# The per-column maximum of a softmax, taken in 32 by 32 blocks on VectorE instead of by five transposes on TensorE

## The chip, the cores and the metric

The kernel runs on one core of one Trainium2 chip. The metric is device time in microseconds of one launch, taken as the median of several runs. One execution was recorded by the hardware profiler, and every duration below comes from that execution.

## The reference, cut to what matters

The whole is one decoder-like layer of three parts (cross-attention with fp8-rounded projections, a small ternary attention with its feed-forward part, a gated feed-forward part). What the change touches is the cross-attention over a long context:

```python
x        : (16, 64, 256)      # 16 batches of 64 queries
ctx_2048 : (16, 1601, 256)    # 16 batches of 1601 context rows
kvx = einsum('bsi,oi->bso', cond, w_kv_x)            # keys and values of the context
kx, vx = split(kvx, 2, axis=-1); kx = _ln(kx ...)    # layer norm over each key head (8 heads of 128)
qx = _ln(_fp8_linear_pertensor(ln_out, wqx, ...))    # 16 query heads, two to a key head
xout = _gqa(qx, kx, vx)                              # softmax(q k / sqrt(128)) v over the 1601 rows
```

The softmax subtracts a maximum, and that maximum is what is computed in another way.

## The kernel before, in words

**Tiles.** The 1024 rows of x are 8 tiles of 128 rows (two batches each). The long attention of a tile is cut into four units: two halves of the heads (hh) times two batches (bb). So there are 32 units, and each walks over 13 chunks of the context (12 of 128 rows and a tail of 65). A unit covers 8 query heads of 64 queries, which makes 512 columns, in four groups g of 128 columns.

**A chunk's way.** `project` (L620) multiplies the context by the key weights on TensorE. ScalarE squares (L555) and splits the keys for a transposing DMA (L647, L651, L661). VectorE sums the squares (`roots`, L560), GpSimd takes the inverse root (L563, L564). `score` (L692, TensorE) makes the scores with context rows on the partitions and the 512 columns along the free axis; ScalarE copies them to a tile P with the inverse root as scale (L702). `running` (L711, VectorE) keeps the running maximum M, a 128 by 512 tile, over the chunks. After the tail chunk `biased_maximum` (L723) adds a bias row to M.

**From M to one maximum for each column.** M still holds 128 partial maxima for each column, one on each partition. `maximum` calls `turned` (L713 to L720): four transposes on TensorE (L717) turn M's four 128 by 128 groups into one PSUM tile tr_m, and VectorE reduces it to 128 by 4, `red` (L719). `out_rows` (L431 to L437) then turns `red` with a fifth transpose (tr_r, L434), ScalarE copies the 4 by 128 result to SBUF (rT, L436), and SyncE's queue writes it to DRAM (rowd, L437). `maximum_in` (L740) reads it back, broadcast to all 128 partitions, as mx. Only the last of the 32 units goes another way: it transposes `red` four more times with broadcast (L734) and uses no DRAM.

**What uses the maximum.** `shifted` (L746, L750, VectorE) adds the negated maximum to each of the 13 stored P tiles, `exponent` (L754, ScalarE) takes the exponential, `accumulate` (L769, TensorE) multiplies by the context. That begins one step after `maximum_in` is issued.

**What sets the order.** A heap of generators with step and rank (`at`, `spawn`, `run`) writes the program in an order laid out by hand; a unit takes 13 steps. The tile framework then places each engine's instructions in a queue of its own, where they run in order, and lets an instruction be moved a little among its neighbours. `ordered("dve", ...)` forbids such a move on VectorE among L560, L711, L723 and L750. `maximum` stands at step 16 of its unit, rank 4.0, after the `project` of that step (rank 2.5) and before its `accumulate` (rank 4.5).

**Buffers.** The score tiles, tr_m, tr_r and most other small PSUM tiles share one tag of three buffers (`tr_tile`, `s_tile`). M has one buffer. `quant_tile()` gives a 128 by 512 scratch tile of two buffers (q_y), used so far by the fp8 rounding, the layer norm of a tile and the query bias on GpSimd (L413).

Of the kernel before, what the change touches and what calls it, by code (L numbers as in the profile page):

```python
# [14 lines left out]
F32 = mybir.dt.float32  # L15
# [5 lines left out]
AX = mybir.AxisListType  # L21
PSUM = bass.MemoryType.PSUM

P = 128
# [49 lines left out]
def body(tc, ctx, a):  # L74
    nc = tc.nc
    V, A, PE, GP = nc.vector, nc.scalar, nc.tensor, nc.gpsimd

    const = ctx.enter_context(tc.tile_pool(name="const", bufs=1))
    small = ctx.enter_context(tc.tile_pool(name="small", bufs=8))
# [6 lines left out]
    dram = ctx.enter_context(tc.tile_pool(name="dram", bufs=2, space=bass.MemoryType.DRAM))  # L86
# [4 lines left out]
    def tr_tile(name, dt=F32):  # L91
        return ps_s.tile([P, 512], dt, tag="s", name=name)
# [7 lines left out]
    def spawn(step, rank, gen):  # L100
        heapq.heappush(heap, (step, rank, next(count), gen))
# [14 lines left out]
    def at(step, rank, fn):  # L116
        def once():
            fn()
            yield 1

        spawn(step, rank, once())
# [22 lines left out]
    ident = const.tile([P, P], F32, tag="ident", name="ident")  # L144
# [85 lines left out]
    def quant_tile():  # L230
        return qp.tile([P, 512], F32, tag="q_y", name="q_y")
# [199 lines left out]
    def out_rows(r, d):  # L431

        tr = tr_tile("tr_r")
        PE.transpose(tr[0:4, 0:P], r, ident)  # L434
        rT = small.tile([4, P], F32, tag="rT", name="rT", bufs=2)
        A.copy(rT, tr[0:4, 0:P])  # L436
        nc.sync.dma_start(out=d, in_=rT)  # L437
# [102 lines left out]
    def behind(ins, other):  # L540

        tc.add_manual_dep(
            ins.ins, other.ins.name,
            mybir.DependencyInfo(mybir.DependencyClass.NoSync, mybir.DependencyReason.DATA), reason="order",
        )

    def ordered(chain, ins):

        if chain in mark:
            behind(ins, mark[chain])  # L550
        mark[chain] = ins
# [41 lines left out]
    def unit(i, hh, bb, base):  # L593
        b = 2 * i + bb
        last, u = b == B - 1 and hh == 1, 4 * i + 2 * hh + bb
        st = {"kh": {}, "kd": {}, "kt": {}, "cxT": {}, "cxN": {}, "ps": {}, "ss": {}, "rs": {}, "kn": {}, "kT": {}, "P": {}, "pT": {}}
# [116 lines left out]
        def turned(what, op):  # L713

            tr = tr_tile("tr_m")
            for g in range(4):
                PE.transpose(tr[:, g * P : (g + 1) * P], st[what][:, g * P : (g + 1) * P], ident)  # L717
            r = small.tile([P, 4], F32, tag="red", name="red")
            V.tensor_reduce(r, tr.rearrange("p (g t) -> p g t", g=4), AX.X, op)  # L719
            return r  # L720

        def biased_maximum():
            ordered("dve", V.tensor_tensor(st["M"], st["M"], st["qb"].rearrange("p h s -> p (h s)"), ALU.add))  # L723

        def maximum():
            r = turned("M", ALU.max)
            if not last:
                st["mxd"] = dram.tile([4, P], F32, tag="rowd", name="rowd", bufs=4)
                out_rows(r, st["mxd"])
                return  # L730

            tr = tr_tile("tr_mb")
            for g in range(4):
                PE.transpose(tr[:, g * P : (g + 1) * P], r[:, g : g + 1].to_broadcast([P, P]), ident)  # L734
            st["mx"] = one.tile([P, 4, P], F32, tag="mx", name="mx", bufs=2)
            A.copy(st["mx"], tr.rearrange("p (g q) -> p g q", g=4))

        def maximum_in():
            st["mx"] = one.tile([P, 4, P], F32, tag="mx", name="mx", bufs=2)
            nc.sync.dma_start(out=st["mx"], in_=st["mxd"].partition_broadcast(P))  # L740

        def shifted(c):
            n, pc = rows_of(c), st["P"][c]
# [12 lines left out]
        def accumulate(c):  # L756


            n = rows_of(c)
            if c == 0:  # L760
                st["acc"] = [ps_acc.tile([P, 512], F32, tag=f"acc{k}", name=f"acc{k}") for k in range(3)]
            pc, cx, acc = st["P"].pop(c), st["cxN"].pop(c), st["acc"]

            for t in acc[:2] if c == 0 else []:
                PE.matmul(t[:, 0:386], lhsT=zeros[:, 0:P], rhs=zeros, start=True, stop=False)
            for g, o, ps in [(0, 0, acc[0][:, 0:257]), (1, 0, acc[1][:, 0:257]), (2, 0, acc[2][:, 0:257]),
                             (3, 0, acc[0][:, 257:385]), (3, P, acc[1][:, 257:386])]:
                w = ps.shape[1]
                PE.matmul(  # L769
                    ps, lhsT=pc[:n, g * P : (g + 1) * P], rhs=cx[:n, o : o + w], start=g == 2 and c == 0,  # L770
                    stop=c == NC - 1 and (g, o) in ((2, 0), (3, 0), (3, P)),
                )
            if c == NC - 1:
                acc = st.pop("acc")
                rv = small.tile([P, 4], F32, tag="rvx", name="rvx", bufs=2)
                pq = one.tile([P, 4, H], F32, tag="pq", name="pq")
                for g, s in enumerate([acc[0][:, 256:257], acc[1][:, 256:257], acc[2][:, 256:257], acc[1][:, 385:386]]):
                    V.reciprocal(rv[:, g : g + 1], s)
                A.activation(pq[:, 0, :], acc[0][:, 0:256], AF.Copy, scale=rv[:, 0:1])
                V.tensor_scalar(pq[:, 1, :], acc[1][:, 0:256], rv[:, 1:2], None, ALU.mult)  # L780
                A.activation(pq[:, 2, :], acc[2][:, 0:256], AF.Copy, scale=rv[:, 2:3])
                V.tensor_scalar(pq[:, 3, P:H], acc[1][:, 257:385], rv[:, 3:4], None, ALU.mult)
                V.tensor_scalar(pq[:, 3, 0:P], acc[0][:, 257:385], rv[:, 3:4], None, ALU.mult)
                st["pq"] = pq
# [15 lines left out]
        for c in range(NC):  # L800
# [20 lines left out]
            at(base + c + 19, 3.7, lambda c=c: exponent(c))  # L821
            at(base + c + 20, 4.5, lambda c=c: accumulate(c))
        at(base + 15, 5.2 + 0.01, biased_maximum)
        at(base + 16 if not last else base + 15, 4.0, maximum)
        if not last:
            at(base + 17, 5.4, maximum_in)
# [429 lines left out]
    for i in range(NT):  # L1256
        base = 52 * i
        for hh in range(2):
            for bb in range(2):
                unit(i, hh, bb, base + 26 * hh + 13 * bb)  # L1260
            spawn(base + 26 * hh + 13 + 34 - 2 + (2, 1)[hh], 6.5, paced("pair", pair_out(i, hh, 4 if i < NT - 1 or hh == 0 else None)))
        ln0, sa0, qx0 = SCHEDULE[i] if i in SCHEDULE else (
            base - 22, [base + o for o in (-15, 0, 8, 21)], [base + o for o in (-16, -7, 15, 18)]
        )
        spawn(ln0, 1.0, paced("ln" if i else "ln_first", ln_tile(i)))
        for p in range(4):
            spawn(sa0[p] - 2, 5.0, paced("sa", self_attention(i, p)))
            spawn(qx0[p] - 2, 3.0, paced("qx", queries(i, p)))
        l0 = base + {NT - 3: 95, NT - 2: 88, NT - 1: 82}.get(i, 90)
        spawn(l0, 4.5, paced("last" if i < NT - 1 else "last_tile", last_parts(i, l0)))  # L1270
# [79 lines left out]
```

## Time and profile before

| | |
|---|---|
| median of 3 runs | 2410.33 us (2405.0 to 2416.17) |
| the profiled execution, its own time | 2408.62 us |
| its span, first to last instruction | 2406.8 us |
| mean granted TensorE clock | 0.991 |
| TensorE matmul, busy | 2333.5 us (97%) |
| TensorE weight load, busy | 1764.1 us (73%) |
| VectorE, busy | 1842.2 us (77%) |
| ScalarE, busy | 1730.2 us (72%) |
| GpSimd, busy | 825.1 us (34%) |

Abbreviations of the profile: PE is TensorE's matmul side, PEld its weight loads, DVE is VectorE, ACT ScalarE, POOL GpSimd, SP SyncE, and SPq SyncE's DMA queue. L717 is line 717 of the kernel before. The matmuls of fp32 operands show as two records each (two passes), the fp32 transposes as one. A matmul's record contains its way through the array, so the records of neighbouring matmuls overlap; how fast TensorE goes is read from start to start, not from durations. "Idle before" is the time in which the group's engine had nothing to do just ahead of it, with the releaser that ended it.

### The profile page before, as it was taken

To read this page: it belongs to the slowest core of one execution; us is meant where nothing else is said; L and a number is where in the kernel's file an instruction comes from. 1 tells how busy PE (TensorE), PEld (TensorE's weight loads), DVE (VectorE), ACT (ScalarE), POOL (GpSimd) and SP (SyncE) were. 2 spreads that over 40 slices of the span, in tenths; PEclk is the share of its full clock that TensorE was granted. 3 is DMA by queue.
4 is the path that set the end of the run, shared out by engine and by line. 5 is a ranking of instruction groups with operands and counts; after the bars stand their busy time and mean duration, and the time that the engine had idled before them with its cause. 6 is when DMAs were issued, how large, how long until landed. Compare 5 with 4: busy or idle time off the path is not lost.

```text
span 2406.8 us, 40362 instructions
## 1 busy us (share of the span) xinstructions
PE 2333.5 (97%) x12541; PEld 1764.1 (73%) x12541; DVE 1842.2 (77%) x4515; ACT 1730.2 (72%) x3789; POOL 825.1 (34%) x1017
## 2 busy tenths in 40 slices
PE   7999999999999999999999999999999999999995
PEld 4577777777777777777777777777777777677774
DVE  7677768878777887687877778777887777876765
ACT  4677777777887777977788777777687777767631
POOL 3333233333343433343433433324434343332200
PEclk9999999999999999999999999999999999999997
DMA  8989868777977689686987769877797767965323
GB/s 262 260 242 254 231 173 242 203 185 188 267 201 199 167 237 232 184 214 181 233 220 193 200 174 256 207 191 189 183 263 199 201 169 190 261 160 140 116 85 110
DMA packets 683661, 485.17 MB, mean 202 GB/s; under 512 B 464476, under 2 KB 592952, under 8 KB 683448
## 3 DMA queue, kind: packets, MB, share of 16 engines
q1 hardware_dynamic: 682904, 481.91, 74.2%
q8 instruction: 100, 1.64, 0.3%
q14 instruction: 113, 0.93, 0.1%
q10 hardware_dynamic: 544, 0.69, 0.1%
HBM read 271.03 MB, written 113.11 MB: 160 GB/s over the span
## 4 chain that ended last, share of the span: by engine, by line
PE 69%; DVE 11%; issue 6%; DMA 5%; POOL 4%; ACT 4%; SPq 1%; ACTq 0%; DVEq 0%; POOLq 0%
PE acc L769 21%; PE ps_k L620 21%; PE s L692 12%; PE po_x L856 2%; PE po_p L325 2%; POOL rsx L564 2%; POOL rs L219 2%; PE ps_q L374 1%; ACT P L702 1%; DMA kd<-kh 1%; DMA wqx<-wqx 1%; DMA kT<-kd 1%; DVE P L750 1%; DVE M L711 1%; PE tr_pc L792 1%
## 5 line engine op out<-in xcount | busy, mean ns | idle before, releaser
L769 PEld LDWEIGHTS acc<-ctxN,P 128*128 128x128 f32 (+1 forms) x4160 | 712.3, 190 | 221.7 <-issue 143.0
L769 PE MATMUL acc<-ctxN,P 128*128 128x257 f32 (+5 forms) x4160 | 803.0, 339 | 4.7 <-DMA ctxN<-in_ctx_n 2.2
L620 PE MATMUL ps_k<-wkx,ctxT 128*128 128x512 f32 x1600 | 759.7, 596 | 8.1 <-DVE wkx L1243 6.4
L702 ACT ACTIVATE P<-s,rsx 128x128 f32<-128x128 f32 x1536 | 441.1, 373 | 159.5 <-PE s L692 144.1
L563 POOL TENSOR_SCALAR vx<-ss 128x4 f32<-128x4 f32 x402 | 145.6, 362 | 1112.5 <-DVE ss L560 785.4
L564 POOL TENSOR_TENSOR rsx<-vx,nhalf 128x4 f32<-128x4 f32 x402 | 471.2, 1172 | 32.8 <-POOL vx L563 0.2
L620 PEld LDWEIGHTS ps_k<-wkx,ctxT 128*128 128x128 f32 x1600 | 276.8, 191 | 201.9 <-issue 185.6
L692 PE MATMUL s<-qx,kT 128*128 128x128 f32 x3072 | 411.7, 277 | 6.3 <-DMA kT<-kd 2.7
L692 PEld LDWEIGHTS s<-qx,kT 128*128 128x128 f32 x3072 | 377.5, 192 | 24.5 <-issue 6.6
L711 DVE TENSOR_TENSOR M<-P,M 128x512 f32<-128x512 f32 (+1 forms) x384 | 264.2, 688 | 156.5 <-ACT P L702 143.6
L647 ACT COPY kh<-ps_k 128x1024 uint16<-128x1024 uint16 x360 | 366.8, 1019 | 3.3 <-DMA kd<-kh 3.1
L754 ACT ACTIVATE P<-P 128x512 f32<-128x512 f32 (+1 forms) x416 | 266.3, 640 | 123.6 <-DVE P L750 121.2
L555 ACT ACTIVATE sq<-ps_k 128x512 f32<-128x512 f32 x402 | 242.8, 604 | 151.3 <-PE ps_k L620 124.6
L560 DVE TENSOR_REDUCE ss<-sq 128x4 f32<-128x512 f32 x402 | 272.3, 677 | 34.1 <-ACT sq L555 32.7
L750 DVE TENSOR_TENSOR P<-P,mx 128x512 f32<-128x512 f32 (+1 forms) x416 | 283.4, 682 | 0.0
L219 POOL TENSOR_TENSOR rs<-ve,nhalf 128x4 f32<-128x4 f32 (+2 forms) x128 | 128.7, 1007 | 278.1 <-DVE ve L218 263.1
L225 DVE TENSOR_SCALAR qn<-qn,mv,rs 128x128 f32<-128x128 f32 x256 | 77.4, 344 | 49.9 <-POOL rs L219 49.0
L303 DVE TENSOR_TENSOR wproj<-wproj,w_hi 128x1024 fp32r<-128x1024 f32 x60 | 72.8, 1216 | 9.0 <-ACT w_hi L302 9.0
L215 DVE BATCH_NORM_STATS2 st<-qn 128x6 f32<-128x128 f32 x256 | 64.5, 271 | 17.8 <-ACT qn L384 17.8
L413 POOL TENSOR_TENSOR q_y<-qn,brow 128x512 f32<-128x512 f32 x32 | 58.5, 1827 | 49.8 <-DVE qn L225 35.2
L302 ACT CAST w_hi<-wproj 128x1024 fp32r<-128x1024 f32 x60 | 63.3, 1056 | 8.5 <-DMA wproj<-wproj 5.4
L325 PE MATMUL po_p<-wproj,cat 128*128 128x256 f32 x272 | 67.0, 293 | 0.0
(234 smaller groups left out, 2871.4 us busy)
## 6 DMA issues: line engine op xcount, KB each, us to landing
kd<-kh SPq DMA_DIRECT2D x375, 256.0 KB
ctxT<-in_ctx SPq DMA_DIRECT2D x192, 256.0 KB
ctxN<-in_ctx_n SPq DMA_DIRECT2D x384, 128.0 KB
wproj<-wproj SPq DMA_DIRECT2D x68, 512.0 KB
wq<-wq SPq DMA_DIRECT2D x32, 512.0 KB
wkv<-wkv SPq DMA_DIRECT2D x32, 512.0 KB
wqx<-wqx SPq DMA_DIRECT2D x32, 512.0 KB
near<-kv SPq DMA_DIRECT2D x248, 64.0 KB
```

Of the source, the lines that this page charges most:

```text
L219: GP.tensor_tensor(rs[:, :g], ve[:, :g], nhalf[:, :g], ALU.pow)
L555: A.activation(sq[:n], ps[:n], AF.Square)
L560: ordered("dve", V.reduce_sum(ss[:n], sq[:n].rearrange("p (g d) -> p g d", g=4), axis=AX.X))
L564: ordered("pool", GP.tensor_tensor(rs[:n], ve[:n], nhalf[:n, 0:4], ALU.pow))
L620: PE.matmul(ps[:n, :], lhsT=st["cxT"][c // 2][:, k, o : o + n], rhs=wkx[:, k, 512 * hh : 512 * (hh + 1)], start=k == 0, stop=k == 1,)
L647: A.copy(t, src.bitcast(U16).rearrange("p (c e) -> p e c", e=2))
L692: PE.matmul(ps[:n, g * P : (g + 1) * P], lhsT=kT[:, g, 0:n], rhs=qxs[i, hh][:, bb, 2 * g : 2 * g + 2, :].rearrange("p h s -> p (h s)"), st ...
L702: A.activation(pc[:, g * P : (g + 1) * P], ps[:, g * P : (g + 1) * P], AF.Copy, scale=rs[:, g : g + 1])
L711: ordered("dve", V.tensor_tensor(st["M"][:n], pc[:n], st["M"][:n], ALU.max))
L750: ordered("dve", V.tensor_tensor(pc[:n], pc[:n], st["mx"][:n].rearrange("p g q -> p (g q)"), ALU.add))
L754: A.activation(pc[:n], pc[:n], AF.Exp)
L769: PE.matmul(ps, lhsT=pc[:n, g * P : (g + 1) * P], rhs=cx[:n, o : o + w], start=g == 2 and c == 0, stop=c == NC - 1 and (g, o) in ((2, 0), ...
```

## The change

VectorE's transpose turns each 32 by 32 block of M in place in the grid, so that the 32 partitions of a block become its 32 free columns. One reduce over the inner 32 then gives r16: for each of four bands of partitions and each of 16 blocks, the maximum of the band, with the 32 columns of the block on the partitions. One transpose on TensorE (r16, 128 by 16) puts the 16 blocks on partitions and the four bands side by side. A last small reduce takes the maximum over the four bands, straight from PSUM into the 16 by 32 tile that the DMA writes to DRAM. The broadcast read back is the same 2 KB for each partition. The last unit is left as it was.

For each of 31 units, four 128 by 128 transposes on TensorE, the 128 by 512 reduce L719 and ScalarE's copy rT go; VectorE gets the transpose and the reduce in `blocks`, directly behind L723 in its ordered chain, and the reduce rmx in `maximum`; the fifth transpose stays, with r16 in place of `red`.

```diff
         def biased_maximum():
             ordered("dve", V.tensor_tensor(st["M"], st["M"], st["qb"].rearrange("p h s -> p (h s)"), ALU.add))
 
+        def blocks():
+            if last:
+                return
+            t = quant_tile()
+            ordered("dve", V.transpose(t, st["M"]))
+            st["r16"] = small.tile([P, 16], F32, tag="r16", name="r16", bufs=2)
+            ordered("dve", V.reduce_max(st["r16"], t.rearrange("p (f t) -> p f t", f=16), axis=AX.X))
+
         def maximum():
+            if not last:
+                tr = tr_tile("tr_m")
+                PE.transpose(tr[0:16, 0:P], st["r16"], ident)
+                r = small.tile([16, 32], F32, tag="rmx", name="rmx", bufs=2)
+                V.reduce_max(r, tr[0:16, 0:P].rearrange("p (b q) -> p q b", b=4), axis=AX.X)
+                st["mxd"] = dram.tile([16, 32], F32, tag="rowd", name="rowd", bufs=4)
+                nc.sync.dma_start(out=st["mxd"], in_=r)
+                return
+
             r = turned("M", ALU.max)
-            if not last:
-                st["mxd"] = dram.tile([4, P], F32, tag="rowd", name="rowd", bufs=4)
-                out_rows(r, st["mxd"])
-                return
...
         def maximum_in():
             st["mx"] = one.tile([P, 4, P], F32, tag="mx", name="mx", bufs=2)
-            nc.sync.dma_start(out=st["mx"], in_=st["mxd"].partition_broadcast(P))
+            nc.sync.dma_start(
+                out=st["mx"].rearrange("p g (f q) -> p (g f) q", f=4), in_=st["mxd"].partition_broadcast(P)
+            )
...
         at(base + 15, 5.2 + 0.01, biased_maximum)
+        at(base + 15, 5.2 + 0.02, blocks)
         at(base + 16 if not last else base + 15, 4.0, maximum)
```

## The prediction

> **What bounds the kernel now.** First the page: busy shares, then the slices.
>
> ```profile
> PE 2333.5 (97%) x12541; PEld 1764.1 (73%) x12541; DVE 1842.2 (77%) x4515; ACT 1730.2 (72%) x3789; POOL 825.1 (34%) x1017
> ...
> PE   7999999999999999999999999999999999999995
> ...
> DVE  7677768878777887687877778777887777876765
> ...
> PEclk9999999999999999999999999999999999999997
> ```
>
> TensorE is busy nearly without a break at an almost full clock, VectorE about three quarters. A busy TensorE may only be waiting in its own pipeline, so second, the waits of TensorE in the stretch from 120 to 2280 us, longest first (total, times, longest):
>
> ```profile
> PE ps_g L1105 <- ACT w_hi L302: 3.0, 3, 1.3
> PE s L692 <- DMA kT<-kd: 2.7, 5, 1.7
> PE acc L769 <- DMA ctxN<-in_ctx_n: 2.2, 3, 0.9
> PE s L692 <- ACT P L702: 2.1, 6, 0.5
> ```
>
> Nothing holds TensorE for more than 3 us in 2160. Third, start to start: successive passes of 128 columns begin 0.109 us apart, of 257 columns 0.216, of 512 columns 0.429. I took each start-to-start gap of the trace, less that interval: the excess is 145 us in the whole span, of which 31 us lie before 120 us and 36 after 2280. Between, it is some 2.2 us in 60, so there TensorE goes at its own pace, and what is taken off its queue is taken off the span.
>
> The Trainium skill ("Perfetto Trace Analysis", Identifying the Most-Contended Engine) warns of just this reading: matmul busy time is a poor measure, weight-load share and the other engines' occupancy a better one. By it VectorE (77%) stands above TensorE (73%), and a change that loads VectorE would lose time (rival C below gives how much). The row here that decides is start to start, and it says TensorE.
>
> Fourth, the timeline of one unit (start, duration, engine, what):
>
> ```profile
> 800.33 0.69 DVE L723 TENSOR_TENSOR M<-M,qb 128x512 f32<-128x512 f32 x1
> ...
> 800.94 0.68 DVE L750 TENSOR_TENSOR P<-P,mx 128x512 f32<-128x512 f32 x1
> ...
> 803.43 0.60 PE L717 MATMUL tr_m<-ident,M 128*128 128x128 f32 x4
> ...
> 803.87 1.03 PE L769 MATMUL acc<-ctxN,P 128*128 128x257 f32 x4
> 804.07 0.69 DVE L719 TENSOR_REDUCE red<-tr_m 128x4 f32<-128x512 f32 x1 [1.65 <-PE tr_m L717]
> ...
> 804.91 0.27 PE L434 MATMUL tr_r<-ident,red 128*4 128x128 f32 x1
> ...
> 805.02 1.04 PE L769 MATMUL acc<-ctxN,P 128*128 128x257 f32 x6
> ```
>
> M is ready at 801.02, TensorE comes to tr_m at 803.43: VectorE is 2.4 us ahead. The four transposes take 803.87 - 803.43 = 0.44 us of the queue. Four passes of acc (4 x 0.216 = 0.86) follow, so tr_r could start at 804.73; it starts at 804.91, since it waits for `red`: 0.17 us of standstill.
>
> **The change part by part.** In the built order of TensorE's queue nothing moves but these instructions (and two key matmuls by some places): one tr_m of 128 by 16 stands where the four stood, and tr_r is gone.
>
> Removed on TensorE: 31 units x 4 x 0.109 = 13.5 us. The new transpose costs what tr_r cost (next start 0.109 us later, stationary 4 columns; 16 columns I take as the same), so the fifth cancels. Also removed: the standstill before tr_r. Summed over the 31 units it is 7.2 us: 2.1 in the first unit, mostly 0.08 or 0.17 in the others. Together 20.7 us.
>
> The new wait: tr_m now needs r16, not M, and behind tr_m in TensorE's queue wait acc and all that follows. The groups that price it (busy, mean ns, idle before and its releaser):
>
> ```profile
> L560 DVE TENSOR_REDUCE ss<-sq 128x4 f32<-128x512 f32 x400 | 271.0, 677 | 33.7 <-ACT sq L555 32.4
> L750 DVE TENSOR_TENSOR P<-P,mx 128x512 f32<-128x512 f32 x384 | 261.7, 682 | 0.0
> L303 DVE TENSOR_TENSOR wproj<-wproj,w_hi 128x1024 fp32r<-128x1024 f32 x60 | 72.8, 1216 | 9.0 <-ACT w_hi L302 9.0
> L719 DVE TENSOR_REDUCE red<-tr_m 128x4 f32<-128x512 f32 x32 | 21.9, 685 | 32.8 <-PE tr_m L717 32.8
> L709 DVE COPY M<-P 128x512 f32<-128x512 f32 x32 | 13.4, 419 | 3.8 <-ACT P L702 3.8
> ```
>
> A VectorE transpose is not in this trace. From below, the fastest row of that shape is the copy L709, 0.42 us; from above, the row with twice the elements, L303, 1.22. I take 0.68 (L750, L711, L560): most rows of 512 fp32 elements have it. The reduce in `blocks` is L560's shape, 0.68. Neighbours on VectorE start 0.08 us before the last one ends (800.33 + 0.69 against 800.94), so each adds 0.60, and tr_r began 0.06 to 0.15 after `red` ended. r16 is thus usable 0.60 + 0.60 + 0.1 = 1.3 us after M.
>
> From the end of L723 to the first tr_m the trace has 0.15 us in two units, 1.53 to 1.54 in five, 1.76 in one, 2.3 or more in 23 (median 3.2). In the first of the two, a weight scaling (0.39) stands between in the built order, so tr_m waits 1.55 us; in the other 1.15. In the five, two small steps (L218, L225; 0.14 and 0.26) come between, so 1.7 is needed against 1.53: 0.2 each, 1.0 in all. The rest waits for nothing. New waits: 3.7 us. With the transpose at 1.22, eight units pay 0.54 more at most, 4.3 us; at 0.42, 1.8 us less.
>
> The Trainium skill ("VectorE: DVE Perf Modes", The three transpose paths; Rules for kernel authors) gives 311 ns for 128 by 128 bf16 on VectorE, sends 128 by 128 transposes to TensorE, and calls the reduce the slowest VectorE operation. Four times 311 ns would be 1.24 us, an estimate, and the time 2398 instead of 2394; the rows show the reduce (677 ns) no slower than the sum of two tensors (682).
>
> VectorE's load: + 0.68 (transpose) + 0.68 (r16) + 0.29 (rmx; L1060 reduces 128 elements in 0.286, L491 256 from PSUM in 0.42) - 0.69 (`red`) = 0.96 us a unit, 30 us over 31, to about 1872. I cost this at nothing. Cover one: VectorE now stands idle 32.8 us in front of `red`, waiting for tr_m; the 1.2 us put in front of that falls into the idle time in the 22 units that have it. Cover two: behind `blocks` in the queue are the shift L750, the sum of squares L560 and the copy L510. From the end of a shift, its exponential allowed for, to its acc there are 8 us in the median, 1.8 at the first percentile; from L510 to its po_s at least 1.6. Both exceed 1.2. If the cover were gone: 31 x 1.2 = 37 us. The new user of q_y has two buffers whose earlier readers are mostly on VectorE itself, ahead of it; one buffer wait on GpSimd's product (1.8 us) would be the most in a unit.
>
> ScalarE loses 31 copies of 0.25 us, 8 us; it is idle 28%, so nothing comes of it. rowd: SyncE's queue waits for rmx instead of rT, behind it stand kd, kT and ctxN. rmx can end about 0.7 us after tr_m starts, rT ended 2.04 us after it (805.47 against 803.43), so that wait gets shorter. The write has 16 rows of 128 bytes for 4 of 512; the read back is 128 by 512 in the built order as before. VectorE waited for mx 4.8 us in all, so the landing has room.
>
> Sum: - 13.5 - 7.2 + 3.7 = - 17 us. The profiled execution took 2408.6 (span 2406.8 and 1.8 around it), so 2391.6; the median lies 1.7 higher: 2410.3 - 17 = 2393.3, say 2394.
>
> **The rivals.**
>
> B, the gain half lost, 2402 us: the transpose takes 1.22 us (4.3 more), and later VectorE steps hold TensorE for another 4, for instance at the s matmuls, which already have 20 us of small waits. For it: the operation's price is unknown. Against: the slacks above. It counts as no change, since 0.5%, 12 us, is about what a measurement of this kernel can tell.
>
> C, slower, 2427 us: VectorE's queue decides after all. Its place is tr_m waiting for r16 and, behind it, everything VectorE hands on late; if the 1.2 us passes whole to TensorE in each unit, it is + 37 - 20.7 = + 16. It decides from 0.67 us a unit on. At tr_m alone that would need r16 3.3 us after M instead of 1.3, since the slacks then cost 21 us. For it: VectorE's 77%, 9 tenths never far. Against: from 120 to 2280 us VectorE is idle 474 us, 16 in each unit.
>
> D, more gained, 2387 us: with tr_r gone, one of the three shared PSUM buffers is asked for less often, and a third of the 20 us at s goes too.
>
> That the change does not do what it says is excluded by the built order: 31 transposes of 16 columns, four old ones in the last unit.
>
> **How the numbers follow.** The forecast 0.55, D 0.11, B 0.24, C 0.10. Half a per cent below the median is 2398.3, above it 2422.4. Faster: forecast and D, 0.66. Same: B, 0.24. Slower: C, 0.10. The range goes from 2385 (D and the cheap transpose) to 2407 (B and its upper bounds); it leaves out C and the rims of B and D, about 0.17. The forecast's own range is 2388 to 2398.
>
> **What would show each step.** Right: TensorE's matmul records fall by 155 - 31 = 124, VectorE's busy time rises to about 1872, the transpose's group shows near 680 ns, L717 has 4 records, and the excess of start-to-start gaps falls by some 3 us net. tr_m waits for r16 in about seven units. Wrong: waits of tr_m for r16 in most units, or new waits of acc or s for P, which would be C; or a transpose group near 1200 ns or beyond.

## The result, and the profile after

The changed kernel takes 2420.35 us (median of 11 runs, 2417.54 to 2424.29); the kernel before took 2409.31 (11 runs, the three above among them). The ratio is 1.0046, with a 95% interval from 1.0038 to 1.0055: about 11 us slower, where 16 us faster was forecast. The time lies above the range of 2385 to 2407. The profiled execution took 2424.29 us (span 2422.5, granted clock 0.988).

First the page of the changed kernel: busy shares, then slices.

```profile
PE 2326.9 (96%) x12417; PEld 1756.8 (73%) x12417; DVE 1864.8 (77%) x4577; ACT 1716.7 (71%) x3758; POOL 841.0 (35%) x1017
...
PE   7899999999999999999999999999999999999995
...
DVE  7577768888877787787877879778887777876764
...
PEclk9899999999999999999999999999999999999997
```

TensorE has 124 records fewer, VectorE is 22.6 us busier, and the clock has an 8 in the second slice. Nothing here says that the kernel is slower: the shares are the same. The groups of VectorE (busy us, mean ns, idle before) price the new steps:

```profile
L729 DVE STREAM_TRANSPOSE q_y<-M 128x512 f32<-128x512 f32 x31 | 21.9, 706 | 0.6
L731 DVE TENSOR_REDUCE r<-q_y 128x16 f32<-128x512 f32 x31 | 21.2, 684 | 0.7
L738 DVE TENSOR_REDUCE rmx<-tr_m 16x32 f32<-16x128 f32 x31 | 8.3, 268 | 4.6 <-PE tr_m L736 4.6
```

(In the profile r16 goes by the name r.) The waits of TensorE from 120 to 2280 us, longest first, are where the loss begins to show:

```profile
PE ps_q L374 <- ACT P L702: 10.4, 5, 2.1
PE tr_m L736 <- DVE r L731: 3.1, 6, 1.4
...
PE sc L486 <- DVE rmx L738: 2.2, 5, 0.4
```

In the kernel before, nothing held TensorE for more than 3 us in this stretch. Now the matmuls of the query projection (ps_q), which the change does not touch, stop five times for 2 us. Start to start, the excess over TensorE's own pace in the whole span went from 145.1 to 174.2 us, 29 more; less the 13.5 us of transposes saved this leaves 15.6, and the two spans differ by 15.7.

The timeline of one unit shows the new steps themselves going as planned:

```profile
808.38 0.69 DVE L723 TENSOR_TENSOR M<-M,qb 128x512 f32<-128x512 f32 x1
809.11 0.71 DVE L729 STREAM_TRANSPOSE q_y<-M 128x512 f32<-128x512 f32 x1
809.86 0.69 DVE L731 TENSOR_REDUCE r<-q_y 128x16 f32<-128x512 f32 x1
810.46 0.68 DVE L765 TENSOR_TENSOR P<-P,mx 128x512 f32<-128x512 f32 x1
811.18 0.63 ACT L769 ACTIVATE P<-P 128x512 f32<-128x512 f32 x1 [2.03 <-DVE P L765]
...
811.49 0.27 PE L736 MATMUL tr_m<-ident,r 128*16 128x128 f32 x1
```

r16 is there 0.94 us ahead of the transpose that needs it. But the shift L765 stands behind it on VectorE, and ScalarE's exponential L769 stood still for 2.03 us until the shift ended. That is the line to follow: over the whole span the wait of the exponential for the shift grew from 121.2 us (before) to 167.3.

**One of the five stops.** The timeline after, around 680 us (start, duration, engine, what, idle before):

```profile
680.47 0.68 DVE L765 TENSOR_TENSOR P<-P,mx 128x512 f32<-128x512 f32 x1
681.19 0.63 ACT L769 ACTIVATE P<-P 128x512 f32<-128x512 f32 x1 [2.23 <-DVE P L765]
681.72 1.12 ACT L702 ACTIVATE P<-s,rsx 128x128 f32<-128x128 f32 x4
...
682.90 0.50 PE L374 MATMUL ps_q<-w_hi,xq 128*128 128x512 f32 x1 [2.09 <-ACT P L702]
```

and the same place in the kernel before:

```profile
671.94 0.68 DVE L750 TENSOR_TENSOR P<-P,mx 128x512 f32<-128x512 f32 x1
672.65 0.63 ACT L754 ACTIVATE P<-P 128x512 f32<-128x512 f32 x1 [0.90 <-DVE P L750]
673.19 1.13 ACT L702 ACTIVATE P<-s,rsx 128x128 f32<-128x128 f32 x4
...
674.38 0.50 PE L374 MATMUL ps_q<-w_hi,xq 128*128 128x512 f32 x1
```

ps_q takes one of the three shared PSUM buffers; a buffer is free once ScalarE has copied its scores out (L702); the copies stand in ScalarE's queue behind the exponential, and that waits for the shift. So a shift for which the exponential waits 1.3 us longer (2.23 against 0.90) holds TensorE for 2 us, though the acc that uses the shifted tile is still far away.

**What else had moved.** In these five tiles (and in one of the last, where no such stop follows) the framework put GpSimd's instructions in another order. GpSimd and the VectorE step that waits for it, after:

```profile
668.72 1.27 POOL L563 TENSOR_SCALAR vx<-ss 128x4 f32<-128x4 f32 x1 [1.61 <-DVE ss L560]
...
670.07 1.04 POOL L564 TENSOR_TENSOR rsx<-vx,nhalf 128x4 f32<-128x4 f32 x1
671.08 1.00 POOL L219 TENSOR_TENSOR rs<-ve,nhalf 128x4 f32<-128x4 f32 x1
672.11 0.34 DVE L225 TENSOR_SCALAR qn<-qn,mv,rs 128x128 f32<-128x128 f32 x1 [1.56 <-POOL rs L219]
```

and before:

```profile
661.76 1.72 POOL L219 TENSOR_TENSOR rs<-ve,nhalf 128x4 f32<-128x4 f32 x1 [3.92 <-DVE ve L218]
663.46 0.24 POOL L563 TENSOR_SCALAR vx<-ss 128x4 f32<-128x4 f32 x1
663.78 1.04 POOL L564 TENSOR_TENSOR rsx<-vx,nhalf 128x4 f32<-128x4 f32 x1
```

The four-wide power L219 of the queries' norm stood ahead of a pair L563, L564; now it stands behind it, and VectorE waits 1.56 us for it at L225, with shifts behind L225 in its queue. VectorE's and ScalarE's instructions also stand in another order in dozens of places, and no run holds those two as they were.

A third difference lies just ahead of the late shift. GpSimd's product L413 runs beside VectorE's subtraction of the maximum from the bias (L746, in the changed kernel L761). After:

```profile
676.91 2.19 POOL L413 TENSOR_TENSOR q_y<-qn,brow 128x512 f32<-128x512 f32 x1 [4.83 <-DVE qn L225]
...
677.28 0.68 DVE L761 TENSOR_TENSOR mx<-qb,mx 128x512 f32<-128x512 f32 x1
679.13 0.69 DVE L417 TENSOR_REDUCE qs<-q_y 128x4 f32<-128x512 f32 x1 [1.17 <-POOL q_y L413]
```

and before:

```profile
668.87 1.27 POOL L413 TENSOR_TENSOR q_y<-qn,brow 128x512 f32<-128x512 f32 x1 [4.05 <-DVE qn L225]
...
669.24 1.45 DVE L746 TENSOR_TENSOR mx<-qb,mx 128x512 f32<-128x512 f32 x1
```

Before, the subtraction is the one that takes longer; after, it is the product, and VectorE waits 1.17 us for it at L417. From the start of the subtraction to the start of the shift it is 2.70 us before (669.24 to 671.94) and 3.19 after (677.28 to 680.47), so 0.49 us of the shift's lateness comes from this. It is the same in all five tiles.

### The profile page after: what moved, and what is told of

Same layout as the page of the kernel before. It is cut to its first block, busy times and chain, and to the rows that moved or that the text cites. A ratio compares the mean times of both kernels' runs of the same rounds, so it can differ in the third digit from the quotient of the medians.

```text
span 2422.5 us, 40061 instructions
## 1 busy us (share of the span) xinstructions
PE 2326.9 (96%) x12417; PEld 1756.8 (73%) x12417; DVE 1864.8 (77%) x4577; ACT 1716.7 (71%) x3758; POOL 841.0 (35%) x1017
## 4 chain that ended last, share of the span: by engine, by line
PE 59%; DVE 15%; issue 7%; POOL 6%; DMA 5%; ACT 5%; SPq 2%; ACTq 0%; DVEq 0%; POOLq 0%
PE ps_k L620 18%; PE acc L784 18%; PE s L692 10%; POOL rsx L564 2%; POOL rs L219 2%; PE po_x L872 2%; ACT P L702 2%; PE po_p L325 2%; DVE P L765 2%; DVE M L711 2%; PE ps_q L374 1%; DMA wqx<-wqx 1%; SPq L1052 1%; DVE qn L225 1%; DVE st L215 1%
## 5 line engine op out<-in xcount | busy, mean ns | idle before, releaser
L563 POOL TENSOR_SCALAR vx<-ss 128x4 f32<-128x4 f32 x402 | 164.5, 409 | 1112.4 <-DVE ss L560 811.5
L702 ACT ACTIVATE P<-s,rsx 128x128 f32<-128x128 f32 x1536 | 439.7, 372 | 139.7 <-PE s L692 127.7
L564 POOL TENSOR_TENSOR rsx<-vx,nhalf 128x4 f32<-128x4 f32 x402 | 464.4, 1155 | 33.2 <-POOL vx L563 0.2
L769 ACT ACTIVATE P<-P 128x512 f32<-128x512 f32 (+1 forms) x416 | 266.7, 641 | 170.0 <-DVE P L765 167.3
L765 DVE TENSOR_TENSOR P<-P,mx 128x512 f32<-128x512 f32 (+1 forms) x416 | 284.2, 684 | 0.0
L219 POOL TENSOR_TENSOR rs<-ve,nhalf 128x4 f32<-128x4 f32 (+2 forms) x128 | 126.3, 988 | 266.8 <-DVE ve L218 253.1
L225 DVE TENSOR_SCALAR qn<-qn,mv,rs 128x128 f32<-128x128 f32 x256 | 77.7, 346 | 57.0 <-POOL rs L219 56.2
L413 POOL TENSOR_TENSOR q_y<-qn,brow 128x512 f32<-128x512 f32 x32 | 63.0, 1969 | 56.6 <-DVE qn L225 37.9
```

The costliest lines, as they stand in the source:

```text
L219: GP.tensor_tensor(rs[:, :g], ve[:, :g], nhalf[:, :g], ALU.pow)
L564: ordered("pool", GP.tensor_tensor(rs[:n], ve[:n], nhalf[:n, 0:4], ALU.pow))
L702: A.activation(pc[:, g * P : (g + 1) * P], ps[:, g * P : (g + 1) * P], AF.Copy, scale=rs[:, g : g + 1])
L765: ordered("dve", V.tensor_tensor(pc[:n], pc[:n], st["mx"][:n].rearrange("p g q -> p (g q)"), ALU.add))
L769: A.activation(pc[:n], pc[:n], AF.Exp)
```

## The experiments

Theories at the start: **L**, the load on VectorE makes shifts and what hangs on them late; **P**, the turn of the shared PSUM buffers changes for the worse; **O**, a changed order of the queues. Each median is compared with runs of the kernel before that were taken beside it; their medians lay at 2408.8 to 2410.7 us.

### e1_cheap_blocks: TensorE's side alone

```diff
-            t = quant_tile()
-            ordered("dve", V.transpose(t, st["M"]))
...
-            ordered("dve", V.reduce_max(st["r16"], t.rearrange("p (f t) -> p f t", f=16), axis=AX.X))
+            ordered("dve", V.tensor_copy(st["r16"], st["M"][:, 0:16]))
```

> The changed kernel, with VectorE's transpose and reduce in `blocks` left out: a copy of M's first 16 columns (128 by 16) stands in r16's place, so the maxima are not those of the columns. Everything else of the change stays: one transpose on TensorE, rmx, the DMAs, the missing PSUM tile tr_r. Theory L (VectorE's 1.3 us ahead of everything else, in stretches where VectorE has no slack, reaches TensorE): the loss goes and TensorE's saving shows, 13.5 us of transposes and some 6 of standstill, so 2385 to 2393 us against 2409 before. Rival P (one PSUM tile fewer shifts the turn in which the three shared buffers are reused): nothing of the loss goes, about 2418. Rival O (the moved order of instructions costs it): between, 2400 to 2420, since the order is made anew.

Measured: 2393.88 us, ratio 0.9938 [0.9918, 0.9957], 16.8 us below the kernel before. That is 16.8 of the 20.7 us that the sum gave to TensorE's side before the new waits, with an interval of about 5 us to each side, and just above the range expected for L. The loss comes with the two VectorE instructions and with the order that the framework then gave the steps around them.

### e2_extra_blocks and e6_extra_transpose: VectorE's side alone

e2 adds the two instructions of `blocks` to the kernel before, with their result unused; e6 adds the transpose alone.

```diff
+        def blocks():
...
+            ordered("dve", V.transpose(t, st["M"]))
...
+            ordered("dve", V.reduce_max(r16, t.rearrange("p (f t) -> p f t", f=16), axis=AX.X))
...
+        at(base + 15, 5.2 + 0.02, blocks)
```

> The kernel before, with the transpose and the reduce to 128 by 16 added on VectorE behind L723 in 31 units, their result unused; the five transposes on TensorE, `red` and rT stay. Theory L: the price of the VectorE work alone, without TensorE's saving of about 20 us: 11 + 20 = 31 us or somewhat less (nobody waits for r16), so 2430 to 2442. Rival P: the PSUM tiles are as before, so 2407 to 2412. The forecast's own view (the load is hidden): 2409 too.

> Half a dose: the kernel before, with VectorE's transpose alone added behind L723 (0.60 us instead of 1.2 a unit), unused; the full dose took 2422 against 2411. Theory L, the cost in proportion: 5 to 6 us, 2414 to 2418. A threshold (the slack swallows up to some amount): below 2413. Rival (it is the transpose instruction, for instance by what it does to GpSimd, and not the time): the whole 11 us, 2420 to 2424.

Measured: e2 2422.01 us, 1.0050 [1.0034, 1.0065]; e6 2410.26, 1.0004 [0.9992, 1.0016]. So 0.6 us more in each unit costs nothing that can be told, 1.2 us cost 11, where 20 to 31 had been expected: in the kernel before there is cover, and it ends between the two. The transposing instruction as such does no harm. Most of e2's loss is at a place that the changed kernel no longer has: tr_r waits for `red`, which now stands behind the additions (its excess goes from 7.2 to 15.2 us). -16.8 and +11.3 would add up to -5.5, not to the +11 measured: something more belongs to the two together.

### e3_second_turn: the PSUM turn given back

```diff
+                tr = tr_tile("tr_r")
+                PE.transpose(tr[0:16, 0:P], st["r16"], ident)
```

> The changed kernel, with r16 transposed twice on TensorE, the second time into a further PSUM tile of the shared tag, from which rmx reads: so the three shared buffers are taken in the same turn as before the change. Theory L: nothing is won back, 31 x 0.109 = 3.4 us are added, 2421 to 2427. Rival P: the loss goes, 2395 to 2405.

Measured: 2425.75 us, 1.0064 [1.0039, 1.0089]. The turn of the buffers is the old one again, and nothing is won back: P falls.

### e4_after_no_bias and e5_before_no_bias: VectorE relieved elsewhere

Both leave out the bias on VectorE (the add to M, L723, and its subtraction from mx); e4 from the changed kernel, e5 from the one before.

```diff
-                V.tensor_tensor(
-                    st["mx"].rearrange("p g q -> p (g q)"), st["qb"].rearrange("p h s -> p (h s)"),
-                    st["mx"].rearrange("p g q -> p (g q)"), ALU.subtract,
-                )
...
-        at(base + 15, 5.2 + 0.01, biased_maximum)
```

> The changed kernel, without the bias: L723 (M + qb) and L746 (qb - mx) on VectorE are taken out and the shift subtracts mx itself. The bias is the same for all context rows of a column, so the softmax does not change. VectorE is relieved of 2 x 0.60 us a unit, about what `blocks` put on it. Theory L: the loss goes, and TensorE's saving shows, 2382 to 2393 us. Rival P: only the little that L723 and L746 cost the kernel before goes, 2412 to 2420.

> The control of the run without bias: the kernel before, five transposes and all, without L723 and L746 on VectorE. It parts two readings of the 2397 us that the changed kernel without bias took. Theory L (VectorE's time ahead of its neighbours is what counts, and TensorE's saving is real once it is covered): the old way of the maximum without bias keeps TensorE's transposes, so it stays at TensorE's pace, 2400 to 2410, and above 2397. Rival (the bias itself was the cost, and the new way of the maximum gives nothing): 2397 or less.

Measured: e4 2397.49 us, 0.9954 [0.9941, 0.9967]; e5 2404.33, 0.9975 [0.9963, 0.9987]. The same relief is worth 5 us to the old way and 23 to the new, and with it the new way is 7 us faster. But GpSimd's order in the five tiles is the old one again in e4, which by itself is worth about 11 of the 23 us (e12 below); that leaves 12 against 5 for the relief of VectorE. So the sign of the change hangs on how full VectorE's queue is and on GpSimd's order. The 2397 us lie above the 2382 to 2393 expected.

### e8_after_late_exp and e9_before_late_exp: the exponential behind the copies

```diff
-            A.activation(pc[:n], pc[:n], AF.Exp)
+            behind(A.activation(pc[:n], pc[:n], AF.Exp), mark["score"])
...
-            at(base + c + 19, 3.7, lambda c=c: exponent(c))
+            at(base + c + 19, 5.6, lambda c=c: exponent(c))
```

> The changed kernel, with ScalarE's exponential (which waits for VectorE's shift) placed behind the copies of the scores (L702) of the same step instead of ahead of them. Theory L with its path (late shift, exponential waits at the head of ScalarE's queue, the copies behind it come late, the score's PSUM buffer stays taken, TensorE stops 2.1 us at ps_q in five tiles): those stops go, some 10 us, 2407 to 2414. Rival (TensorE's stops come by another way, for instance by the maximum's round trip over DRAM): 2417 to 2423.

> The control of the late exponential: the kernel before with the same move on ScalarE. Theory L: it has no such stops to lose, so 2405 to 2413; a drop by 10 us here too would say that the move helps any kernel of this form and tells nothing of the change.

Measured: e8 2485.35 us, 1.0310 [1.0286, 1.0335]; e9 2502.23, 1.0386 [1.0364, 1.0408]. As a measure of the loss this misfired: the move itself costs 65 to 93 us, since acc now waits for the exponential.

```profile
PEld acc L786 <- ACT P L771: 161.1, 243, 2.3
```

One thing can still be read: once acc has the wait, the new way is 17 us ahead of the old. The five stops at ps_q are gone from e8, but that does not show that they come by way of the exponential: GpSimd's order in the five tiles is the old one in e8 too, and that alone takes most of each stop away (e12 below).

### e12_after_pool_order and e15_before_pool_swap: GpSimd's order alone

e12 (first diff) holds L219 ahead of the pair in the changed kernel. Its edit acts after every norm, so beside the five tiles it moves L219 ahead in more than a dozen places where the kernel before has it behind: GpSimd's order in e12 is not that of the kernel before. Only e15 is the five swaps and nothing else. e15 (second) puts it behind the pair in the five tiles of the kernel before (`px` is the power L564 of the second root after the norm); in both, VectorE's and ScalarE's orders are those of the kernel that was edited.

```diff
+        mark["norm"] = GP.tensor_tensor(rs[:, :g], ve[:, :g], nhalf[:, :g], ALU.pow)
...
+        if "norm_before" in mark:
+            behind(vx, mark["norm_before"])
```

```diff
+            if mark["norm"][1] == WHICH and mark["norms"] in SWAPS:
+                behind(mark["norm"][0], px)
```

> The changed kernel with GpSimd's order held as it was before the change: the four-wide power of the queries' norm (L219) stands ahead of the pair L563, L564 in the five tiles where the change let them swap places. The other engines' orders are those of the changed kernel. Theory order: the swap makes the five stops of TensorE at ps_q (about 2 us each, at 680, 970, 1260, 1549 and 1832 us), and part of the half-clock time after them; the stops vanish (excess at ps_q from 11.7 to 3 us or less) and the median falls by 10 to 14 us, to 2406 to 2412. Theory load alone: the late shift behind blocks causes them whatever GpSimd's order; the stops stay and the median is 2418 to 2423.

> The kernel before, with the four-wide power of the queries' norm (L219) put behind the next pair L563, L564 on GpSimd in the same five tiles as in the changed kernel, and nothing else: the orders of the other engines are those of the kernel before. Theory A, the swap is enough: the five stops of TensorE at ps_q come (excess at ps_q from 2.4 to 8 us or more) and the median rises by 6 to 12 us, to 2416 to 2422. Theory B, the swap and the longer queue of VectorE are both needed: the exponential ahead of ps_q comes later by at most a microsecond, still in time; the excess at ps_q stays under 5 us and the median is 2408 to 2414.

Measured: e12 2409.65 us, 0.9997 [0.9988, 1.0007]; e15 2418.31, 1.0033 [1.0022, 1.0045]. The order is worth 11 us in the changed kernel and 9.5 in the kernel before, where it is the only difference. TensorE's waits from 120 to 2280 us in e12:

```profile
PE ps_q L374 <- ACT P L707: 2.4, 5, 0.8
```

and in e15:

```profile
PE ps_q L378 <- ACT P L711: 8.6, 5, 1.7
```

The five places, read in all four kernels, show how the causes meet. L413 is GpSimd's product, in us; a wait of 0.14 is too short to be listed in the views:

| | L413 | exponential waits for the shift | ps_q waits |
|---|---|---|---|
| before, all five | 1.27 | 0.90 | 0.14 |
| VectorE's load (e12), three places | 1.27 | 1.05 | 0.28 |
| VectorE's load (e12), two places, 680 us among them | 2.18 | 1.54 | 0.77 |
| GpSimd's order alone (e15), all five | 1.27 | 1.74 | 1.72 |
| changed kernel, all five | 2.19 | 2.23 | 2.09 |

The order is enough by itself. The load by itself adds little here, 0.15 us to the exponential's wait. Where the product is the one that takes longer, the exponential waits 0.49 us more in e12 (1.54 against 1.05), and the changed kernel and e15 differ by as much (2.23 against 1.74). That does not hang on the load alone: in e1, without the two instructions, three of the five products are long, in e6 none. What decides it was not found.

The five waits are only some 8 of e12's 11 us. A lower clock overlaps with them: the granted clocks of the runs average 0.9887 in the changed kernel, 0.9905 in e12 and 0.9915 in e15, which is at most 4 us between the first two. The rest is spread and was not traced further. Beside the changed kernel and e15, only e3 has the swapped order; e1, e2, e4, e6 and e8 have the old one. That is the larger part of why load and saving did not add up; the first unit is the rest.

### e14_after_first_old: the first unit by the old way

```diff
         def blocks():
-            if last:
+            if last or u == 0:
...
         def maximum():
-            if not last:
+            if not last and u > 0:
```

> As e12_after_pool_order, and the first of the 31 units takes its maximum in the old way (four transposes of M, one reduce, one more transpose). Theory start-up: the changed kernel loses 7 us between 72 and 121 us, since in the first unit the transpose waits 2.9 us for r16 and half-clock windows follow; with the old way there this comes back, and the median is 5 to 9 us below that of e12. Theory noise of the start: what half-clock windows the start has does not hang on the first unit; the median is within 3 us of e12's.

Measured: 2404.11 us, 0.9977 [0.9966, 0.9989], 5.5 us below e12. By the scatter of the two sets of runs that is good to about 3 us, so it is clear of zero, but the other theory's 3 us is not quite excluded. In the changed kernel the first transpose stands still longer than any other:

```profile
101.99 0.37 PE L736 MATMUL tr_m<-ident,r 128*16 128x128 f32 x1 [2.78 <-DVE r L731]
```

In that stretch the projection weights are still being prepared on VectorE (L286, L244, L312 are among its instructions from 96 to 100 us), so VectorE is not ahead of TensorE there. Matched instruction by instruction with the kernel before, TensorE in the profiled executions is 6.4 us behind at 125 us in e12, and 0.6 in e14.

### e10_after_bias_gone and e11_before_bias_gone: a faster version

Both leave out the whole making of the bias: its side product (L413), its reduce, its transposes and DMAs.

```diff
-        out_rows(qs, qbs[i, p // 2][4 * (p % 2) : 4 * (p % 2) + 4, :])
-        fact("qb", i, p // 2)
...
-    spawn(-8, 1, bias_rows())
```

> The changed kernel without the whole machinery of the bias that adds one constant to a row of scores and so leaves the softmax as it is (L409, L413, L417, the transposes and DMAs that carry it, L723, L746). Theory load: VectorE and GpSimd lose more work than in e4_after_no_bias (2397), TensorE loses 16 more transposes (2 us); 2380 to 2394. Theory order: with other work gone the scheduler may place steps anew, so it may also come out at 2397 or above.

> The kernel before without the same machinery. Theory load: the old way has no VectorE loss to get back beyond what e5_before_no_bias (2404) showed; 2397 to 2403, and the new way (e10_after_bias_gone) is 7 to 17 us faster than this.

Measured: e10 2382.18 us, 0.9884 [0.9871, 0.9896], the fastest of all; e11 2392.14, 0.9932 [0.9917, 0.9947]. On a VectorE that is 70 us less busy (1794.1 and 1771.4 us) the new way is 10 us faster than the old. The old way gained more than expected (2397 to 2403). GpSimd's order in the five tiles is the old one in both.

## Why the prediction was wrong

The medians, each against the kernel before measured beside it, make a chain from the forecast to the result:

| step | from, to | us |
|---|---|---|
| TensorE's side | before, e1 | -16.8 |
| VectorE's load in 30 units, with the order made anew | e1, e14 | +11.2 |
| the first unit | e14, e12 | +5.5 |
| GpSimd's order | e12, changed kernel | +11.0 |
| sum | | +11 |

The intervals of the ratios are about 2 to 5 us to each side, so the single terms are good to some microseconds. Between e1 and e14 VectorE's and ScalarE's orders differ in dozens of places too; what of the second term is the load and what the order was not parted.

**Right.** 124 records fewer; VectorE busy 1864.8 us (forecast 1872); the transpose 706 ns (taken 680), so the lower and upper rows were not needed; tr_m waits for r16 in seven units, as said; and the saving on TensorE, -13.5 - 7.2 = -20.7 us in the sum before the new waits, -16.8 in e1 with an interval of about 5. That this is also the -17 of the whole sum is chance, since e1 has no wait for r16. The span of e1's profiled execution is 15.1 us shorter, so the 13.5 us of transposes are there and little of the standstill: the 7 us went at tr_r and came back elsewhere.

**Mis-sized.** r16 was to be usable 1.3 us after M; the median is 1.47. The 0.08 us by which neighbours overlap holds for independent instructions; M, transpose and reduce each need the one before, and start 0.03 us after its end. The first unit was one of the two priced at 1.55 and 1.15 us, and waits 2.8. The excess at tr_m is 9.3 us, against 8.8 at tr_m and tr_r together before: the forecast of -7.2 + 3.7 became +0.5. rmx was to end 0.7 us after tr_m starts; the median is 1.2 and the longest 3.4, since other steps stand ahead of it on VectorE, and five matmuls of sc wait for its buffer (2.2 us).

**The step that failed** is VectorE's load, "I cost this at nothing", and in it cover two. It measured 11.2 us in 30 units and 5.5 in the first. Cover two followed three steps behind `blocks` to their own results; the shift's slack was taken through its exponential to its acc, 8 us in the median. But VectorE hands on more than these three, and the exponential has another reader of its time: everything behind it in ScalarE's queue. Over the span the exponential waits 122.0 us for the shift in e1 and 154.3 in e14. The copies L702 behind it free PSUM buffers, and from the shift by way of exponential, copies and buffer to ps_q the kernel before had no slack at the five places: 0.15 us more wait of the exponential (e12, three places) lengthens the wait of ps_q by 0.14. The 11.2 us is small waits at many places, some of which wait for VectorE directly: between the profiled executions of e1 and e14, whose spans differ by 8.8 us, the excess grows by 4.5 us at tr_aq, 3.5 at sc (for rmx), 3.1 at the tail scores, 3.1 at ps_q, 2.8 at tr_m (for r16), and falls by 5.2 at acc.

The second failure is a sentence that was true and too narrow: in the built order "of TensorE's queue nothing moves but these instructions". GpSimd's queue did move, in five places that matter, and VectorE's and ScalarE's in dozens. The move on GpSimd is as large a term as the load: 9.5 us by itself (e15), 11 in the changed kernel (e12). Why the framework chose the other order was not tried.

Rival C had the right side and half of the mechanism (VectorE's queue, new waits behind it). Its price let the whole 1.2 us of each unit pass to TensorE, +16 in all; +11 were measured, about as much of it from GpSimd's order, which no rival named, as from the load. The wait for r16 at tr_m, which it put first, is 6 us. That its number comes near is in part luck. The Trainium skill ("Perfetto Trace Analysis", Identifying the Most-Contended Engine), which by its measure puts VectorE first, had the sign; the start-to-start reading was right that TensorE sets the pace, and said nothing of how little slack the others had.

## What to carry to other kernels

When a change lengthens one engine's queue, follow each late step through every in-order queue that it enters: an instruction that waits at the head of ScalarE's queue delays all behind it, and what these free (here PSUM buffers), long before its own result is needed. Compare the built order of every engine, the idle ones too; a swap of small GpSimd steps in five places cost nearly as much here (9.5 us) as 1.2 us of new VectorE work in each of 30 units (11.2). And a saving on the pacing engine is paid in full only if the engine that takes the work over has room in the stretch where it takes it, so try the change again after relieving that engine.

## What the runs showed of the hardware

**A clock that halves without a long pause.** The windows of the changed kernel around the stop at 1549 us (columns: window, length, busy of PE, PEld, VectorE, ScalarE, GpSimd, then granted clock, DMA share, GB/s):

```profile
1548.70:1552.10 3.40, 1.32 (x7) 0.98 (x6) 2.27 (x6) 2.71 (x7) 1.26 (x2) 1.00 0.94 218
1552.10:1555.50 3.40, 3.40 (x5) 1.34 (x4) 2.81 (x10) 1.57 (x3) 0.00 (x0) 0.50 0.70 217
```

After a 3.4 us window in which TensorE was busy 1.32 us, the next is granted at half clock, and the key matmuls in it run at half speed (four passes of 512 columns take 3.37 us from start to start; at full clock they begin 0.429 apart). The Trainium skill ("TensorE: Matmul & The Clock Gate", What's actually happening) gives an idle window of about 3.4 us as the cause; here a stop of 2.08 us was enough. It is not always: the stops at 1549 and 1832 us are followed by a half-clock window, those of the same length at 680, 970 and 1260 are not. In all the profiled execution of the changed kernel spent 58.1 us at half clock, that of the kernel before 41.7, so up to 8 us of the difference between these two. e3, with the same stops, spent 44.4. Over all runs the lower clock stays: the granted clock averages 0.9887 in the 11 runs of the changed kernel and 0.9912 in the runs of the kernel before that were taken beside the experiments. With a clock that is either full or half, as in these traces, that is some 12 us more at half clock, an estimate, and at most 6 of the 11 us lost. The swap alone (e15) loses its 9.5 us at 0.9915, without a lower clock, so the stops cost time by themselves.

**GpSimd's product and VectorE's subtraction stretch each other.** In the five tiles the product L413 takes 1.27 us and the subtraction beside it 1.45 (before, and e15), or the product 2.19 and the subtraction 0.68 (the changed kernel); the subtraction starts 0.37 us after the product in both cases. The median of L413 went from 1.29 to 2.18 us with no change to it, since 18 of 32 instead of 13 are the long ones, and the five are these. The Trainium skill ("GPSIMD Engine Reference", Specifications) says that the two share their interfaces to SBUF, with contention where VectorE's instruction has two inputs there, which fits; it does not say which of the two gives way.
